# Order of the four matmul groups inside one attention score tile of a two-layer block

## The chip, the cores and the metric

The kernel runs on one core of a Trainium2 chip. The metric is the time on the device, in microseconds (us), from launch to end, as the median of several runs. Smaller is better. Instructions run on five engines side by side: TensorE (PE; its weight loads are listed as PEld), VectorE (DVE), ScalarE (ACT), GpSimd (POOL) and SyncE (SP), which only issues transfers.

## The reference, cut to what matters

The program is a block of two layers on x of shape (8, 512, 256). The change lies in the attention of the first layer, with 16 heads of 64 dimensions:

```python
q = _rmsnorm((x @ Wq).reshape(B, T, H, D), q_rms_w)
k = _rmsnorm((x @ Wk).reshape(B, T, H, D), k_rms_w)
v = (x @ Wv).reshape(B, T, H, D)
gate = softplus(einsum('bthd,hd->bht', k, u_n) / sqrt(D))
dist = maximum(idx[:, None] - idx[None, :], 0)
bias = -dist[None, None] * omega_eff[None, :, None, None] * gate[:, :, None, :]
bias = where(causal[None, None], bias, -inf)
scores = einsum('bihd,bjhd->bhij', q, k) * scale + bias
attn = softmax(scores, axis=-1)
y = einsum('bhij,bjhd->bihd', attn, v).reshape(B, T, H * D)
return y @ Wproj
```

The rest of the block (layer norms, an expert layer with routing, a small two-matrix layer and a block-sparse feed-forward layer) is untouched. Scores are a sum of three terms: q by k, a bias linear in the distance, and a causal mask.

## The kernel before, in words

**Stages.** A first stage (until about 137 us of the span) normalises and transposes all eight sequences and routes tokens to experts. The middle stage (137 to 1283 us) holds attention, the output projection and the experts. The last (to the end) is the second layer.

**Attention.** It runs over 32 groups: eight sequences times four groups of four heads. For each group `produce` projects q and k (L456), v and the gate (L464), scales and transposes q and k (L514), and builds the gate rows gT (L639 and its copy at L646). Then `attend(u)` runs over 256 units: 64 pairs of heads times four blocks of 128 query rows, taken in the order 2, 0, 3, 1. Block i looks at w = 128(i + 1) key columns, so that units have 384, 128, 512 and 256 columns.

**One unit.** `scores` fills a PSUM tile `sc` of two banks, one bank for each head of the pair. Head 0 has its operands on partitions 0 to 63 and head 1 on 64 to 127, so a matmul of one head uses half of the array's rows (64*128 in the profile), and the two heads can run side by side. The three terms are accumulated in PSUM by four groups of matmuls, each of one matmul per head:

- the bias rows, L678: constant rows `bst` (bf16) as weights, `gT` (bf16) moving, w columns. The bias is carried by a few rows of each half;
- the mask in two groups, L683: constant selectors `mst` (bf16) as weights and large negative steps `mmv` (bf16) moving. The first (c = 0) covers the 128 columns of the diagonal block, the second (c = 1) its last 64 columns;
- q by k, L688: q transposed (fp32) as weights and k transposed (fp32) moving, w columns. Every fp32 matmul appears in the profile as two records.

The group that comes first has `start=True`, which overwrites what was in the bank; the last has `stop=True`.

After the scores, VectorE takes the row maximum (L694), ScalarE the exponentials with row sums (L700), VectorE the reciprocal (L707), GpSimd the division (L710), TensorE the transposes of the result, full-array matmuls of 128 columns (L723), and ScalarE and VectorE copy those out (L731, L733). After four units of a pair, TensorE multiplies by v (L756). `output` (L786) projects finished sequences.

**What sets the order.** A planner written in the kernel (`Plan`) decides the order. Each operation states its engine, a cost in ns, what it depends on, a due time, and which buffers it takes and returns. `emit` simulates the engines with these costs and calls the functions in the order that results; each engine then runs its own queue in that order. All ten score matmuls of one unit are a single operation:

```python
sc = op("PE", 110 + 270 * (i + 1), scores, s.ready, u, acq=["sc"], rel=last, mode="R")
```

Its mode is "R" (half of the rows); other TensorE operations have "F" (full array), "C" (half of the columns) or "E" (experts), and the planner adds 93 ns where the mode changes. There are two score buffers (`sc`). A unit's scores need the group's gT and transposed q and k (`s.ready`), and a free score buffer, returned by the second exponential.

**Elsewhere in the profile.** In the last layer, L1195 is an fp32 matmul that uses 64 rows (64*128) of 256 columns between full-array matmuls of L1197, and L1183 is a bf16 matmul on 16 rows (16*128) of 512 columns between full-array fp32 matmuls of L1179.

Of the kernel before, what the change touches and what calls it, by code (L numbers as in the profile page):

```python
# [139 lines left out]
def tile_two_layer_block(  # L140
# [26 lines left out]
    nc = tc.nc  # L167
# [27 lines left out]
    bst = const.tile([P, NPR, T], BF16, tag="bst", name="bst")  # L195
# [4 lines left out]
    for h in range(2):  # L200
        k = slice(h * D, (h + 1) * D)
# [96 lines left out]
    with tc.tile_pool(name="pa", bufs=2) as pa, tc.tile_pool(name="pa1", bufs=1) as pa1:  # L298
# [13 lines left out]
        for half in range(B // BPG):  # L312
            lg = sc_tile(f"lg_{half}")
            xns = []
            for i in range(BPG):
# [11 lines left out]
                for dc in range(NC):  # L327
                    nc.tensor.matmul(
                        lg[i * E : (i + 1) * E, :], gwT[:, dc, :], xT[:, dc, :],
                        start=(dc == 0), stop=(dc == NC - 1),  # L330
# [38 lines left out]
            for i in range(BPG):  # L369
                for dc in range(NC):  # L370
                    col = (i * NC + dc) * E
                    for t in range(NT):
# [4 lines left out]
                            start=(t == 0), stop=(t == NT - 1),  # L377
# [50 lines left out]
    with tc.tile_pool(name="pb", bufs=2) as pb, tc.tile_pool(name="pb1", bufs=1) as pb1:  # L428
# [231 lines left out]
        def attend(u):  # L660

            pr, c = divmod(u, NT)
            n, q = divmod(pr, NPR)
            i = ORDER[c]
            s = grp[n]
            n0 = i * P
            w = n0 + P
# [4 lines left out]
            m = Grp()  # L672
            heads = [(h, slice(h * D, (h + 1) * D)) for h in range(2)]

            def scores():
                m.sc = ps_sc.tile([P, 2, T], F32, tag="sc", name=f"sc_{u}")
                for h, k in heads:
                    nc.tensor.matmul(  # L678
                        m.sc[:, h, :w], bst[k, q, n0:w], s.gT[k, :w], start=True, stop=False
                    )  # L680
                for c in range(2):
                    for h, k in heads:
                        nc.tensor.matmul(  # L683
                            m.sc[:, h, n0 + c * D : w], mst[k, c, :], mmv[k, c, c * D :],
                            start=False, stop=False,
                        )
                for h, k in heads:
                    nc.tensor.matmul(  # L688
                        m.sc[:, h, :w], s.qT[k, q, n0:w], s.kT[k, q, :w], start=False, stop=True
                    )  # L690

            def most():
                m.nm = pb.tile([P, 2], F32, tag="nmx", name=f"nm_{u}", bufs=3)
# [40 lines left out]

            last = ["qk", "gT"] if u % NU == NU - 1 else []
            sc = op("PE", 110 + 270 * (i + 1), scores, s.ready, u, acq=["sc"], rel=last, mode="R")
            mx = op("DVE", 69 + 2.07 * w, most, [sc], u + 0.1, acq=["nm"])
            e0 = op("ACT", 254 + 0.83 * w, lambda: expo(0), [mx], u + 0.2, acq=[f"pr{i}", "sums"])
# [228 lines left out]
    with tc.tile_pool(name="pc", bufs=2) as pc, tc.tile_pool(name="pc1", bufs=1) as pc1:  # L967
# [98 lines left out]
        for dc in range(NC):  # L1066
            for k in range(NC):
# [3 lines left out]
                    start=(k == 0), stop=(k == NC - 1),  # L1071
# [177 lines left out]
```

## Time and profile before

| | |
|---|---|
| median of 3 runs | 1664.84 us (1663.77 to 1667.19) |
| profiled execution | 1665.2 us, its span 1663.5 us |
| mean granted TensorE clock | 0.977 |
| TensorE busy, 0 to 137 us | 91.33 us |
| TensorE busy, 137 to 1283 us | 1132.63 of 1146.00 us |
| TensorE busy, 1283 to 1663.5 us | 369.15 of 380.50 us |
| score matmuls L688: records, busy | 1024, 201.0 us |
| mask matmuls L683: records, mean | 512 of 128 columns, 216 ns; 512 of 64 columns, 189 ns |
| bias matmuls L678: records, mean by columns | 128 each: 225 ns (128), 279 (256), 333 (384), 386 (512) |

How to read it: the span runs from the first to the last instruction of one profiled execution. A line such as "L678 PE MATMUL sc<-gT,bst 64*128 64x384 bf16" names the source line, the engine, the output and its inputs, the part of the array in use (rows*columns), and the moving operand (rows x columns and type). Lengths of matmul records are modelled and overlap with the following ones, since the array is pipelined: the distance from one start to the next is what TensorE really spends. LDWEIGHTS records are the loads of weights into the array, which can lie beside a running matmul.

### The profile page before, as it was taken

To read this page: it belongs to the slowest core of one execution; us is meant where nothing else is said; L and a number is where in the kernel's file an instruction comes from. 1 tells how busy PE (TensorE), PEld (TensorE's weight loads), DVE (VectorE), ACT (ScalarE), POOL (GpSimd) and SP (SyncE) were. 2 spreads that over 40 slices of the span, in tenths; PEclk is the share of its full clock that TensorE was granted. 3 is DMA by queue.
4 is the path that set the end of the run, shared out by engine and by line. 5 is a ranking of instruction groups with operands and counts; after the bars stand their busy time and mean duration, and the time that the engine had idled before them with its cause. 6 is when DMAs were issued, how large, how long until landed. Compare 5 with 4: busy or idle time off the path is not lost.

```text
span 1663.5 us, 26380 instructions
## 1 busy us (share of the span) xinstructions
PE 1593.1 (96%) x9416; PEld 933.3 (56%) x9416; DVE 922.3 (55%) x2682; ACT 700.5 (42%) x1918; POOL 590.7 (36%) x1082
## 2 busy tenths in 40 slices
PE   4789999999999999999999999999999899999999
PEld 1455555655665565565556556655655655555555
DVE  5537666666666665665666676666666332333331
ACT  1115554455446544544555454455545121222221
POOL 4016444444444444534444444444444100000000
PEclk9679999999999999999999999999999899999999
DMA  8000113032011302211130122123014000000000
GB/s 267 26 4 1 52 53 106 8 105 81 30 58 52 103 11 81 77 57 58 52 103 7 58 79 80 46 67 103 7 58 138 14 10 13 14 13 13 13 13 16
DMA packets 72914, 89.26 MB, mean 54 GB/s; under 512 B 5016, under 2 KB 55984, under 8 KB 72784
## 3 DMA queue, kind: packets, MB, share of 16 engines
q1 hardware_dynamic: 71552, 86.87, 16.0%
q8 instruction: 75, 1.23, 0.3%
q10 hardware_dynamic: 1232, 0.71, 0.2%
q14 instruction: 55, 0.45, 0.1%
HBM read 83.11 MB, written 4.19 MB: 52 GB/s over the span
## 4 chain that ended last, share of the span: by engine, by line
PE 89%; DVE 3%; ACT 1%; issue 1%; POOL 0%; ACTq 0%; DVEq 0%; POOLq 0%
PE pq L456 13%; PE sc L688 9%; PE pp L723 9%; PE y L756 9%; PE ph L1179 7%; PE py L1197 7%; PE po L786 7%; PE pv L464 6%; PE pqk L514 4%; PE sc L678 4%; PE peo L925 2%; PE ph L867 2%; PE sc L683 1%; PE ph L1183 1%; PE py L1195 1%; PE ph L861 1%
## 5 line engine op out<-in xcount | busy, mean ns | idle before, releaser
L710 POOL TENSOR_SCALAR pr<-pr,rinv 128x384 f32<-128x384 f32 (+3 forms) x512 | 265.9, 532 | 424.8 <-DVE rinv L707 244.3
L700 ACT ACTIVATE pr<-sc,nm 128x384 f32<-128x384 f32 (+3 forms) x512 | 266.2, 527 | 139.3 <-DVE nm L694 73.9
L241 POOL TENSOR_TENSOR rsqk<-ss,nhalf 128x8 f32<-128x8 f32 x128 | 210.8, 1647 | 146.5 <-DVE ss L491 140.9
L456 PE MATMUL pq<-wqk_sb,xnT 128*128 128x512 f32 x512 | 247.4, 606 | 3.3 <-DVE gl L482 3.3
L694 DVE TENSOR_REDUCE nm<-sc 128x2 f32<-128x768 f32 (+3 forms) x256 | 209.8, 823 | 73.4 <-PE sc L688 70.7
L723 PE MATMUL pp<-ident,pr 128*128 128x128 f32 x1280 | 218.9, 281 | 4.9 <-DVE prT L733 2.7
L723 PEld LDWEIGHTS pp<-ident,pr 128*128 128x128 f32 x1280 | 147.7, 141 | 122.0 <-issue 60.0
L688 PE MATMUL sc<-kT,qT 64*128 64x384 f32 (+3 forms) x1024 | 201.0, 471 | 0.0
L731 ACT COPY prT<-pp 128x384 f32<-128x384 f32 (+3 forms) x256 | 107.2, 426 | 156.4 <-PE pp L723 154.5
L733 DVE COPY prT<-pp 128x384 f32<-128x384 f32 (+3 forms) x256 | 123.4, 487 | 84.2 <-PE pp L723 81.2
L756 PE MATMUL y<-prT,v 128*64 128x256 f32 (+3 forms) x1024 | 152.2, 439 | 0.7 <-ACT prT L731 0.7
L464 PE MATMUL pv<-wvg_sb,xnT 128*128 128x260 f32 x512 | 136.4, 389 | 8.0 <-DVE osb L938 6.8
L456 PEld LDWEIGHTS pq<-wqk_sb,xnT 128*128 128x128 f32 x512 | 87.9, 192 | 85.3 <-issue 70.7
L1179 PE MATMUL ph<-xT,w1T 128*128 128x512 f32 x256 | 128.7, 620 | 0.0
L756 PEld LDWEIGHTS y<-prT,v 128*64 128x64 f32 x1024 | 68.4, 136 | 105.0 <-issue 63.4
L1197 PE MATMUL py<-w2T,hT 128*128 128x256 f32 x512 | 124.0, 388 | 0.0
L786 PE MATMUL po<-wp_sb,yT 128*128 128x256 f32 x512 | 116.4, 381 | 0.0
L1105 POOL TENSOR_TENSOR xres<-x,b_bc 128x1024 f32<-128x1024 f32 x8 | 18.8, 2344 | 265.1 <-DVE x L1098 265.1
L471 ACT ACTIVATE sq<-pq 128x512 f32<-128x512 f32 x128 | 76.3, 596 | 81.4 <-PE pq L456 78.6
L464 PEld LDWEIGHTS pv<-wvg_sb,xnT 128*128 128x128 f32 x512 | 89.0, 191 | 36.8 <-issue 14.6
L1197 PEld LDWEIGHTS py<-w2T,hT 128*128 128x128 f32 x512 | 93.3, 190 | 25.7 <-issue 15.3
L488 DVE TENSOR_REDUCE ss<-sq 128x8 f32<-128x512 f32 x128 | 87.4, 683 | 35.7 <-ACT sq L471 34.9
(187 smaller groups left out, 2067.7 us busy)
## 6 DMA issues: line engine op xcount, KB each, us to landing
ew<-in_L_ffn_w_dram SPq DMA_DIRECT2D x128, 512.0 KB
xt<-in_L_attn_x_dram SPq DMA_DIRECT2D x8, 512.0 KB
xr<-in_L_attn_x_dram SPq DMA_DIRECT2D x32, 128.0 KB
out_dram<-ot SPq DMA_DIRECT2D x32, 128.0 KB
raw<-in_L_ffn_w_dram SPq DMA_DIRECT2D x4, 512.0 KB
wqk_sb<-in_L_attn_Wq_dram SPq DMA_DIRECT2D x2, 512.0 KB
wqk_sb<-in_L_attn_Wk_dram SPq DMA_DIRECT2D x2, 512.0 KB
wvg_sb<-in_L_attn_Wv_dram SPq DMA_DIRECT2D x2, 512.0 KB
```

Source lines behind the costliest of these rows:

```text
L241: nc.gpsimd.tensor_tensor(r, src, nhalf[:, :n], ALU.pow)
L456: nc.tensor.matmul(s.pq[t], xnT[b][:, dc, cols], wqk_sb[:, dc, g, :], start=(dc == 0), stop=(dc == NC - 1),)
L464: nc.tensor.matmul(s.pv[t][:, : GW + HG], xnT[b][:, dc, cols], wvg_sb[:, dc, g, :], start=(dc == 0), stop=(dc == NC - 1),)
L688: nc.tensor.matmul(m.sc[:, h, :w], s.qT[k, q, n0:w], s.kT[k, q, :w], start=False, stop=True)
L694: nc.vector.tensor_reduce(m.nm, m.sc[:, :, :w], AX.X, ALU.max, negate=True)
L700: nc.scalar.activation(m.p[:, h, :], m.sc[:, h, :w], AF.Exp, bias=m.nm[:, h : h + 1], accum_out=m.sums[:, h : h + 1],)
L710: nc.gpsimd.tensor_scalar(m.p[:, h, :], m.p[:, h, :], m.rinv[:, h : h + 1], 1.0, ALU.mult, ALU.mult)
L723: nc.tensor.transpose(m.pt[h][:, d * P : (d + 1) * P], m.p[:, h, j * P : (j + 1) * P], ident)
L756: nc.tensor.matmul(pp.yp[h * D : (h + 1) * D, j * P :], s.v[j][:, hh * D : (hh + 1) * D], pp.tri[:, h, j : j + 4 * (NT - 1 - j) + 1 : 4, : ...
L786: nc.tensor.matmul(o.po[:, :C], yT[b * nk + k][:, t * P : (t + 1) * P], wp_sb[:, k, :], start=(k == 0), stop=(k == nk - 1),)
L1179: nc.tensor.matmul(ph, w1T[:, dc, k * P : (k + 1) * P], s.xT[:, dc, :], start=(dc == 0), stop=False,)
L1197: nc.tensor.matmul(py[:, :C], hT[:, c, cols], w2T[:, c, :], start=False, stop=(c == NFC - 1),)
```

## The change

Inside `scores` the order of the groups becomes q by k, first mask (c = 0), bias rows, second mask (c = 1). `start=True` moves to q by k, and `stop=True` to the second mask. The operands, the shapes and the number of matmuls stay as they are, and so do the operation's cost, due time, mode and buffers in the planner, and with them the order of operations on every engine. Later lines have their numbers raised by two.

```diff
                 for h, k in heads:
                     nc.tensor.matmul(
-                        m.sc[:, h, :w], bst[k, q, n0:w], s.gT[k, :w], start=True, stop=False
+                        m.sc[:, h, :w], s.qT[k, q, n0:w], s.kT[k, q, :w], start=True, stop=False
                     )
                 for c in range(2):
                     for h, k in heads:
                         nc.tensor.matmul(
                             m.sc[:, h, n0 + c * D : w], mst[k, c, :], mmv[k, c, c * D :],
-                            start=False, stop=False,
-                        )
-                for h, k in heads:
-                    nc.tensor.matmul(
-                        m.sc[:, h, :w], s.qT[k, q, n0:w], s.kT[k, q, :w], start=False, stop=True
-                    )
+                            start=False, stop=bool(c),
+                        )
+                    if c == 0:
+                        for h, k in heads:
+                            nc.tensor.matmul(
+                                m.sc[:, h, :w], bst[k, q, n0:w], s.gT[k, :w],
+                                start=False, stop=False,
+                            )
```

## The prediction, made before the changed kernel ran

> **What bounds the kernel now.** I read the busy shares first, then the chain that ended last, then TensorE's waits inside the attention stage, and last single matmuls there in order of time. From the page, parts 1 and 4:
>
> ```profile
> span 1663.5 us, 26380 instructions
> PE 1593.1 (96%) x9416; PEld 933.3 (56%) x9416; DVE 922.3 (55%) x2682; ACT 700.5 (42%) x1918; POOL 590.7 (36%) x1082
> ...
> PE 89%; DVE 3%; ACT 1%; issue 1%; POOL 0%; ACTq 0%; DVEq 0%; POOLq 0%
> ```
>
> TensorE holds 89% of the chain, and the other engines have slack. The scores run from 137 to 1283 us. In the table of that one stretch TensorE is busy 1132.63 of 1146.00 us, at a granted clock of 1.00, so what one score unit takes on TensorE goes into the end time almost unabated. The view of TensorE's waits in this stretch has two lines that concern this change:
>
> ```profile
> PE pv L464 <- DVE osb L938: 6.8, 7, 1.0
> PE sc L678 <- ACT pr L700: 1.5, 4, 0.4
> ```
>
> The columns are total us, times and longest. Score units wait 1.5 us in all, always for a score buffer to come free; they never wait for the bias rows gT. Starting with q by k can therefore save no wait.
>
> Now one unit of 384 columns, in order of time (start us, length us; "x2" are the two heads, which run side by side in the two halves of the array):
>
> ```profile
> 613.71 0.27 PE L723 MATMUL pp<-ident,pr 128*128 128x128 f32 x1
> 613.92 0.34 PE L678 MATMUL sc<-gT,bst 64*128 64x384 bf16 x2
> 614.09 0.25 PE L683 MATMUL sc<-mmv,mst 64*128 64x128 bf16 x4
> 614.17 0.57 PE L688 MATMUL sc<-kT,qT 64*128 64x384 f32 x2
> 614.58 0.49 PE L688 MATMUL sc<-kT,qT 64*128 64x384 f32 x2
> 615.00 0.70 PE L464 MATMUL pv<-wvg_sb,xnT 128*128 128x260 f32 x2
> ```
>
> Lengths are modelled and overlap, so I count from start to start, and below use the trace's start stamps to the nanosecond. Each fp32 matmul has two records. The first q by k record lasts 0.57, the second 0.48 (0.49 in this merged line): something holds up the first. The view of weight loads in the same stretch shows it:
>
> ```profile
> 613.91 0.10 PEld L678 LDWEIGHTS <-bst 64*128 64x128 bf16 x2 [0.17 <-issue]
> 613.93 0.26 PEld L683 LDWEIGHTS <-mst 64*128 64x128 bf16 x4
> 614.15 0.30 PEld L688 LDWEIGHTS sc<-kT,qT 64*128 64x128 f32 x4
> ```
>
> The fp32 load for q by k starts at 614.15, when the last mask matmul has only just begun. That matmul streams 27 ns, so most of the load stands uncovered. The bias load starts only at 613.91, 0.20 us after the last transpose began, although it was next in the queue: at the passage from the full array to half arrays nothing is loaded ahead.
>
> **What the skill says.** TensorEngine Tiling (Array Packing), section Key Properties: changing the tiling mode drains the engine. The trace agrees: 613.71 to 613.916 is 205 ns where two transposes in a row start 107 ns apart, so 98 are lost; from the last q by k record to the next full-array matmul it is 413 ns against a streaming time of 320, that is 93, or 97 counted from the first head of the pair. TensorE: Matmul & The Clock Gate, section LDWEIGHTS: a load takes its columns over 1.2, which for 128 is 107 ns; the first fp32 matmul after a passage is 104 to 107 ns longer than the second throughout this trace. The same page, Weight-path perf modes: the fast load is for 128 weights that aren't fp32. Here the bf16 bias record of 128 columns has a mean of 225 ns against 216 for a mask record of the same form, so its uncovered load costs about 10. The same page, Back-to-back issue gap: columns over 2.4. In this trace bf16 transposes of 128 start 55.5 ns apart, and an fp32 record counts twice.
>
> **The change part by part.** No instruction is added or removed: ten matmul records per unit, in the order q by k, first mask, bias, second mask. Pure streaming stays 2x2w + w + 128 + 64 columns, 880 ns for w = 384, and cancels. What lies around it changes. Before, bias start to next start is 549, 813, 1080 and 1346 ns (medians for 128, 256, 384, 512 columns); less streaming of 347, 613, 880 and 1147, that leaves 200 to 202, with these parts (ns):
> - 13, first load (bias, bf16) and the second head's offset;
> - 3 from mask to mask, 2 from mask to q by k;
> - 86, q by k's load behind the 27 ns mask (the 0.57 against 0.48);
> - 97, drain to the next step.
> With the 98 of the drain on entry it is 298.
>
> After:
> 1. Entry drain. Full to half array with fp32 first is in the trace at the last layer's L1195 (64*128, 256 columns): 309 ns from the L1197 before it, less 213, gives 96. So 2 less.
> 2. First load, now q by k's fp32 one: the same L1195 shows it uncovered.
>
> ```profile
> L1195 PE MATMUL py<-aw2T,gT x64: 376/428/480, 1338.0 to 1656.3; 64*128 64x256 f32 x64
> ```
>
> 480 is the first record and 376 the second. From first to second start it is 320 ns, less 213: 107 where the bias load cost 13.
>
> 3. q by k's load behind a mask goes: 86 to 0.
> 4. q by k to first mask, mask to bias, bias to second mask: 3 each. The mask's bf16 load lies behind a q by k record of at least 107 ns, the bias load behind a 53 ns mask and the second mask's behind the bias. From fp32 to bf16 inside half-array mode no record exists; in full mode it is 109 against 107 (transpose to bf16 transpose), so I take 3. If this passage isn't free, see the second rival.
> 5. Drain to the next step after a bf16 mask. The trace has L1183 (16*128 bf16, 512 columns), 314 to the next start, less 213, less its own uncovered load of 13: 88, and 3 for the second head make 91. With nothing taken off it is 101, with the second head 104. I take 94, plus 2 for the 27 ns matmul ahead. The next step's load stays uncovered before and after, since the passage loads nothing ahead; that the step before it is now short costs nothing.
> Sum: 96 + 107 + 9 + 2 + 94 = 308, so 10 ns more per visit, with ends 305 (+7) and 318 (+20).
>
> The plan's order has two units in succession ten times, where only the first pays for the entry and the second's q by k hides behind a short mask as before. So 256 units make 246 visits: 246 x 10 = 2.5 us, ends 1.7 and 4.9.
>
> **Others who are touched.** The operations' order on every engine is the same, for costs and due times in the plan are unchanged; no DMA moves. The buffer wait (1.5 us) passes to the first q by k record, and the wait for gT, at a group's first unit, to the bias behind it: behind both stands only TensorE's own queue, and neither was ever late by more than the 0.4 shown. The maximum on VectorE starts when the last record of the unit is written, some 10 ns later; its own idle time before TensorE's scores doesn't hold the chain.
>
> The profiled execution took 1665.2 us (span 1663.5 and 1.7 around it), the median shown is 1664.84. So 1665.2 + 2.5 = 1667.7 for such an execution, and 1667.3 on the scale of the medians. A measurement of this kernel can't tell less than about 0.2%, 3.3 us, from no change.
>
> **Rivals.**
> - *The load of q by k goes ahead during the drain* (faster). Then the 107 are gone: 246 x 97 = 23.9 us less than before, 1641. For it: it would be a different load from the bias's. Against it: L1195 after full-array work, and every first fp32 record of the other modes (pv at 615.00 lasts 0.49 where later ones last 0.38). A smaller gain through gT's late arrival has no wait to live on.
> - *fp32 to bf16 in half-array mode isn't seamless* (slower). At the place q by k to first mask, the mask's load might not be hidden: 13 ns x 256 = 3.3 us, together 1670.6. If the passage drains as a mode change does, 96 x 256 = 24.6 us, together 1691.9. It decides from about 4 ns per unit on, since 0.8 us more brings the sum to 3.3. For it: no record shows the passage. Against it: the full-array one at 2 ns.
> - *The exit after a short bf16 matmul is the dear one*: the upper end above, 246 x 20 = 4.9, 1669.7; it is in the forecast's own range.
>
> **How the numbers follow.** The forecast, a trade of one uncovered load for another at 1666.5 to 1669.7, has a chance of 0.70, of which 0.48 are within 0.2%, 0.20 slower, 0.02 faster by scatter. The second rival has 0.20 (0.15 small, 0.05 a full drain), 0.19 of it slower and 0.01 within. The first has 0.10, with unforeseen gains: 0.08 faster, 0.02 within. Sum: faster 0.10, same 0.51, slower 0.39. The time is 1667.3. The range leaves out the full drain and the gain of a hidden load: 1663.7 to 1671.5, with about 2 us of the scatter shown (1663.77 to 1667.19) at either end.
>
> **What would show it.** In the new profile's first unit: the q by k pair directly after the 0.20 us gap, its first record about 105 ns longer than the second (0.59 and 0.48 at 384 columns); the bias record of 384 columns down from 333 by some 10; unit start to next start about 1092 at 384. Step 4 is wrong if q by k's second record to the mask takes over 325 ns at 384 columns, step 5 if second mask to next start is outside 118 to 134, step 2 if both q by k records are alike. If TensorE's waits in the stretch 137 to 1283 us change from 13 us by more than 2, the reason isn't on TensorE, and the forecast misses it.

## The result, and the profile after

| | before | changed |
|---|---|---|
| median, first comparison (7 runs each) | 1664.98 us | 1670.41 us |
| ratio | | 1.0031 (1.0019 to 1.0043) |
| median, second comparison (59 and 22 runs) | 1666.56 us | 1670.20 us |
| ratio | | 1.0023 (1.0014 to 1.0032) |
| profiled execution, span | 1663.5 us | 1668.1 us |

The change makes the kernel slower by 0.2 to 0.3%: 5.4 us in the first set of runs, 3.6 us between the medians of the second and larger one. The forecast was 1667.3 us; the time is inside the range and the direction of the 2.5 us was right, but it is more than what had been summed. By the forecast's own line of 0.2%, no change had the larger chance (0.51, against 0.39 for slower): the first comparison lies beyond this line, and the second, at 0.23% (0.14 to 0.32), isn't clear of it.

The page of the changed kernel, parts 1 and 4:

```profile
span 1668.1 us, 26384 instructions
PE 1597.7 (96%) x9416; PEld 953.1 (57%) x9416; DVE 921.9 (55%) x2682; ACT 700.5 (42%) x1918; POOL 590.8 (35%) x1082
...
PE 89%; DVE 3%; ACT 1%; issue 1%; POOL 0%; ACTq 0%; DVEq 0%; POOLq 0%
```

TensorE has 4.6 us more busy time, and the span is 4.6 us longer. The weight loads (PEld), which can lie beside a matmul, take 19.8 us more; the other engines' busy times are the same within 0.4 us. TensorE's waits in the stretch 137 to 1283 us (total us, times, longest):

```profile
PE pv L464 <- DVE osb L940: 6.8, 7, 1.0
...
PE sc L678 <- ACT pr L702: 1.2, 3, 0.4
```

They are those of before, and the score buffer's wait has passed to q by k. So the time has gone into TensorE's own work. The unit of 384 columns that the prediction took apart, now in the changed kernel, as the timeline shows it, matmuls first and weight loads below:

```profile
614.69 0.27 PE L725 MATMUL pp<-ident,pr 128*128 128x128 f32 x1
614.90 0.59 PE L678 MATMUL sc<-kT,qT 64*128 64x384 f32 x2
615.32 0.49 PE L678 MATMUL sc<-kT,qT 64*128 64x384 f32 x2
615.64 0.22 PE L683 MATMUL sc<-mmv,mst 64*128 64x128 bf16 x2
615.70 0.33 PE L689 MATMUL sc<-gT,bst 64*128 64x384 bf16 x2
615.86 0.20 PE L683 MATMUL sc<-mmv,mst 64*128 64x64 bf16 x2
615.99 0.71 PE L464 MATMUL pv<-wvg_sb,xnT 128*128 128x260 f32 x2
```

```profile
614.89 0.30 PEld L678 LDWEIGHTS sc<-kT,qT 64*128 64x128 f32 x4 [0.16 <-issue]
615.32 0.10 PEld L683 LDWEIGHTS <-mst 64*128 64x128 bf16 x2
615.65 0.10 PEld L689 LDWEIGHTS <-bst 64*128 64x128 bf16 x2 [0.22 <-issue]
615.70 0.10 PEld L683 LDWEIGHTS <-mst 64*128 64x128 bf16 x2
615.99 0.52 PEld L464 LDWEIGHTS pv<-wvg_sb,xnT 128*128 128x128 f32 x3 [0.18 <-DVE ss L488]
```

The first fp32 load starts at 614.89, together with its matmul and not with the transpose before it: all of it lies open, that is, no matmul runs beside it, and the first q by k record takes 0.59 us. The masks' and the bias's loads start while a matmul runs ahead of them; from start to start only 2 to 3 ns are added to the streaming in this unit. From the first start to the next step's start it is now 1094 ns where it was 1080; at 128, 256 and 512 columns the medians are 563, 827 and 1360 where they were 549, 813 and 1346.

Laid over each other operation by operation, the two traces show where the 4.6 us arise. The score visits are 3.54 us longer in sum (246 x 14.4 ns), and the transposes, most of which lead into them, 0.72 us shorter (those of L723 0.62, those of q and k 0.10). Together 2.82 us. The beginning of the last layer adds 0.28 us, and the first stage is 0.20 us shorter. Another 1.69 us come at one place in the last layer, which the change doesn't touch. The table of stages shows this place for the 4 us around it in the changed kernel (us, then busy time of PE, PEld, DVE, ACT, POOL, then the granted clock, DMA share, GB/s):

```profile
1414.00:1418.00 4.00, 4.00 (x11) 2.96 (x11) 2.09 (x17) 1.22 (x2) 0.00 (x0) 0.57 0.00 0
```

The granted clock is at half for 3.4 us there, which is 1.7 us lost. The same work in the profile before, which comes 3 to 5 us earlier, lies within these 12 us and ran at a clock of 1.00:

```profile
1405.40:1417.40 12.00, 12.00 (x59) 8.37 (x58) 4.19 (x23) 1.54 (x2) 0.00 (x0) 1.00 0.07 23
```

### The profile page after: what moved, and what is told of

The parts are those of the page before. It is cut to its first block, busy times and chain, and to the rows that moved or that the text cites. A ratio compares the mean times of both kernels' runs of the same rounds, so it can differ in the third digit from the quotient of the medians.

```text
span 1668.1 us, 26384 instructions
## 1 busy us (share of the span) xinstructions
PE 1597.7 (96%) x9416; PEld 953.1 (57%) x9416; DVE 921.9 (55%) x2682; ACT 700.5 (42%) x1918; POOL 590.8 (35%) x1082
## 4 chain that ended last, share of the span: by engine, by line
PE 89%; DVE 3%; ACT 1%; issue 1%; POOL 0%; ACTq 0%; DVEq 0%; POOLq 0%
PE pq L456 13%; PE sc L678 11%; PE pp L725 9%; PE y L758 9%; PE ph L1181 7%; PE py L1199 7%; PE po L788 7%; PE pv L464 6%; PE pqk L514 4%; PE sc L689 2%; PE peo L927 2%; PE ph L869 2%; PE sc L683 1%; PE ph L1185 1%; PE py L1197 1%; PE ph L863 1%
## 5 line engine op out<-in xcount | busy, mean ns | idle before, releaser
L678 PE MATMUL sc<-kT,qT 64*128 64x384 f32 (+3 forms) x1024 | 207.1, 481 | 1.4 <-ACT pr L702 1.4
```

Of the source, the lines that this page charges most:

```text
L678: nc.tensor.matmul(m.sc[:, h, :w], s.qT[k, q, n0:w], s.kT[k, q, :w], start=True, stop=False)
```

## The experiments

Two questions were open: whether the half-clock stretch belongs to the change, and whether the score units' part comes from uncovered weight loads, as summed, or from something else in the new order (the change from fp32 to bf16, the bias behind a short mask, the exit after a short matmul). All kernels below compute the same sums in another order of the four groups. In all of them `start=True` stands at the first group and `stop=True` at the last. The edits are shown against the kernel before, cut to the lines that say where a group stands.

**Both kernels once more, in one set of runs on one chip.**

The kernel before:

> The kernel before once more, as its own comparison. Theory A (the change costs only what its score units show, 12 ns on each of 246 visits, 2.9 us; the rest of the 5.4 us measured is one more stretch of 3.4 us at half clock in the last layer, 1.7 us, that comes or stays away by chance of phase): 1664 to 1667, a ratio of 1.000, and some of its runs with a mean clock of 0.976 and a span about 1.7 us above those with 0.977. Theory B (the change itself brings the half-clock stretch or another cost outside the score units): all of its runs at 0.977, spans within 1 us.

The changed kernel:

> The changed kernel once more. Theory A: spans with clock 0.977 about 1666.3 to 1667.3, those with 0.976 about 1.7 us more; runs of equal clock 2.9 us, to 3.8 us, above the kernel before. Theory B: nearly all at 0.976, and a difference above 4.5 us also at equal clock.

Measured: 1666.52 us for the repeated kernel before, ratio 0.9999 (0.9991 to 1.0007); 1670.20 for the changed one, ratio 1.0023. Sorted by each run's mean clock:

| mean clock | before (59 runs) | changed (22 runs) | difference |
|---|---|---|---|
| 0.975 | 1667.94 (6 runs) | 1669.91 (2) | 1.97 |
| 0.976 | 1667.03 (33) | 1670.39 (12) | 3.36 |
| 0.977 | 1665.63 (6) | 1668.63 (2) | 3.00 |
| 0.980 and 0.981, against 0.982 | 1662.13 (14) | 1664.93 (3) | 2.80, but the clocks aren't equal |

Three more runs of the changed kernel lie at 0.974 (1673.55 and 1674.19) and 0.972 (1675.47); none of the 59, nor of the 22 of the repeated kernel before, is under 0.975.

A stretch of 3.4 us at half clock lowers the mean over 1665 us by 0.001, and costs 1.7 us where TensorE never waits. At equal clock, as far as three digits show it, 2.0 to 3.4 us remain, the 2.0 from two runs alone. That is near the 3.1 of the score visits, their transposes and the beginning of the last layer.

What Theory B expected of the kernel before isn't so: its repeated runs lie at 0.976 (12 runs, 1666.95 us), 0.977 (5, 1665.66) and 0.981 (5, 1662.26), so that other clocks come without the change too. But the change isn't cleared of the stretch at 1414 us. It stands at this place in two of the four traces of kernels that begin with q by k, and in none of the four that begin with the bias. The repeated kernel before was profiled at 0.976 without it: there the clock from 20 to 50 us is 0.73 where it was 0.76, and 1.36 of the 1.55 us by which its span is longer arise before 137 us. So the place that Theory A names, the last layer, isn't the rule for the kernel before. Whether the order of the groups makes the stretch at 1414 us more likely stays open.

The repeated changed kernel was profiled at 0.977, with a clock of 1.00 from 1405 to 1425 us. Its score visits are 3.54 us longer once more, and the transposes 0.72 shorter. Its span is 3.9 us above that of the profile before, at the same mean clock: 2.8 us in the middle stage, 0.3 at the beginning of the last layer, and 0.7 in the first stage, which the change doesn't touch.

**Bias first, then q by k, then both masks.** The changed lines:

```diff
-                for c in range(2):
-                    for h, k in heads:
-                        nc.tensor.matmul(
-                            m.sc[:, h, n0 + c * D : w], mst[k, c, :], mmv[k, c, c * D :],
...
-                        m.sc[:, h, :w], s.qT[k, q, n0:w], s.kT[k, q, :w], start=False, stop=True
+                        m.sc[:, h, :w], s.qT[k, q, n0:w], s.kT[k, q, :w], start=False, stop=False
...
+                        m.sc[:, h, n0 : w], mst[k, 0, :], mmv[k, 0, :],
+                        start=False, stop=False,
...
+                        m.sc[:, h, n0 + D : w], mst[k, 1, :], mmv[k, 1, D:],
+                        start=False, stop=True,
```

> Order bias, q by k, first mask, second mask: it has the passage from fp32 to bf16 and the exit after a short bf16 mask, as the changed kernel has, but starts with the quick bf16 load, and the fp32 load lies behind the bias record. Account of uncovered loads (107 ns less what the matmul ahead streams): 13 at the start; q by k's load uncovered by 54 ns at 128 columns, by 0 at 256, 384, 512. Units shorter than before by about 27 ns at 128 columns and 81 at the others: start to next start about 522, 732, 999, 1265 ns; 64 x (27 + 3 x 81) = 17.3 us less, about 1647.7, ratio 0.990. Rival (the cost of the change lies in the passage from fp32 to bf16 or in the exit after a short matmul, not in the first load): it remains slower than before or equal, 1665 to 1668.

Measured: 1649.45 us, ratio 0.9896 (0.9883 to 0.9909). Start to next start is 522, 733, 997 and 1264 ns; the score visits are 17.28 us shorter in sum, where 17.3 were expected. The rival falls: this order has both the passage from fp32 to bf16 and the short last matmul, and is 1% faster than the kernel before. The same unit in its trace, matmuls and loads:

```profile
606.75 0.27 PE L727 MATMUL pp<-ident,pr 128*128 128x128 f32 x1
606.96 0.34 PE L678 MATMUL sc<-gT,bst 64*128 64x384 bf16 x2
607.13 0.48 PE L682 MATMUL sc<-kT,qT 64*128 64x384 f32 x2
```

```profile
606.96 0.36 PEld L682 LDWEIGHTS sc<-kT,qT 64*128 64x128 f32 x4
```

q by k's load starts at 606.96 with the bias matmul, 0.17 us ahead of its own matmul, and the first q by k record takes 0.48, as the second does. The groups by form show where the cover is too short (the figures are busy us and mean ns of a q by k record; first the kernel before, then this one):

```profile
L688 PE MATMUL sc<-kT,qT 64*128 64x512 f32 x256 | 70.8, 630 | 0.0
L688 PE MATMUL sc<-kT,qT 64*128 64x128 f32 x256 | 29.9, 312 | 0.0
```

```profile
L682 PE MATMUL sc<-kT,qT 64*128 64x512 f32 x256 | 65.4, 589 | 0.0
L682 PE MATMUL sc<-kT,qT 64*128 64x128 f32 x256 | 28.2, 298 | 0.0
```

At 512 columns the mean is 589, the length of the second record alone, where it was 630. At 128 it is 298, where an unhindered record has 272: half of 53, since only the first of two records waits.

**Bias, first mask, q by k, second mask.**

```diff
-                for c in range(2):
-                    for h, k in heads:
-                        nc.tensor.matmul(
-                            m.sc[:, h, n0 + c * D : w], mst[k, c, :], mmv[k, c, c * D :],
...
-                        m.sc[:, h, :w], s.qT[k, q, n0:w], s.kT[k, q, :w], start=False, stop=True
+                        m.sc[:, h, n0 : w], mst[k, 0, :], mmv[k, 0, :],
...
+                        m.sc[:, h, :w], s.qT[k, q, n0:w], s.kT[k, q, :w], start=False, stop=False
...
+                        m.sc[:, h, n0 + D : w], mst[k, 1, :], mmv[k, 1, D:],
+                        start=False, stop=True,
```

> Order bias, first mask, q by k, second mask: the fp32 load of q by k lies behind a mask of 128 columns (53 ns) where the kernel before has one of 64 (27 ns). Account of uncovered loads: 107 - 53 = 54 uncovered, with the pair's offset 57 or so, where it was 86 behind 27 ns; the exit after a bf16 mask is 2 to 3 dearer. Units 27 to 30 ns shorter than before at every width: about 521, 785, 1052, 1318 ns, together 6.9 to 7.4 us less, ratio 0.9957. Rival (a load behind any short mask is lost alike, and what helped the order with q by k second was only the number of changes between formats): units as before within 5 ns, ratio 1.000.

Measured: 1659.64 us, ratio 0.9957 (0.9943 to 0.9971). Start to next start is 522, 786, 1053 and 1319 ns; in sum 6.78 us less than before, where the medians of the runs are 6.3 us apart. The rival falls. The groups by form of this kernel:

```profile
L687 PE MATMUL sc<-kT,qT 64*128 64x512 f32 x256 | 69.0, 617 | 0.0
L687 PE MATMUL sc<-kT,qT 64*128 64x128 f32 x256 | 28.2, 298 | 0.0
```

617 against 589 and 298 against 272: 26 to 28 on the mean, so 53 to 56 ns on the first record at either width. What lies open is set by the matmul just ahead, not by the unit's size.

**q by k, bias, then both masks.**

```diff
-                        m.sc[:, h, :w], bst[k, q, n0:w], s.gT[k, :w], start=True, stop=False
...
+                        m.sc[:, h, :w], s.qT[k, q, n0:w], s.kT[k, q, :w], start=True, stop=False
...
-                        m.sc[:, h, :w], s.qT[k, q, n0:w], s.kT[k, q, :w], start=False, stop=True
+                        m.sc[:, h, :w], bst[k, q, n0:w], s.gT[k, :w], start=False, stop=False
...
+                        m.sc[:, h, n0 : w], mst[k, 0, :], mmv[k, 0, :],
+                        start=False, stop=False,
...
+                        m.sc[:, h, n0 + D : w], mst[k, 1, :], mmv[k, 1, D:],
+                        start=False, stop=True,
```

> Order q by k, bias, first mask, second mask: the bias is moved behind q by k, the rest as in the changed kernel. Account of uncovered loads: the first load costs 107 as in the changed kernel, every later one is hidden; units equal to the changed kernel's within 3 ns (563, 827, 1094, 1360), time within 1 us of it. Rival (the bias behind a 53 ns mask pays for its place): units 10 to 13 ns shorter, 2.5 to 3.3 us less than the changed kernel.

Measured: 1669.98 us, ratio 1.0020 (1.0012 to 1.0027); at a clock of 0.976 it is 1670.10 (16 runs) against the changed kernel's 1670.39. The medians of the units are 563, 827, 1094 and 1360, the same as the changed kernel's to the nanosecond. The bias's place behind the short mask costs nothing.

**q by k, both masks, bias last.**

```diff
-                        m.sc[:, h, :w], bst[k, q, n0:w], s.gT[k, :w], start=True, stop=False
...
+                        m.sc[:, h, :w], s.qT[k, q, n0:w], s.kT[k, q, :w], start=True, stop=False
...
-                        m.sc[:, h, :w], s.qT[k, q, n0:w], s.kT[k, q, :w], start=False, stop=True
+                        m.sc[:, h, n0 : w], mst[k, 0, :], mmv[k, 0, :],
...
+                        m.sc[:, h, n0 + D : w], mst[k, 1, :], mmv[k, 1, D:],
...
+                        m.sc[:, h, :w], bst[k, q, n0:w], s.gT[k, :w], start=False, stop=True
```

> Order q by k, first mask, second mask, bias: as the changed kernel, but the last matmul before the exit is the bias with all its columns in place of a mask of 64. Account of uncovered loads: units as in the changed kernel within 3 ns (563, 827, 1094, 1360), since nothing is loaded ahead at the exit and the first load costs 107 as there. Rival (a short last matmul makes the exit dear): units 5 to 10 ns shorter than the changed kernel's, most at 512 columns.

Measured: 1670.67 us in a single run, at a clock of 0.975, so that only its trace is used. Units of 563, 827, 1094 and 1360 again, although the last matmul has up to 512 columns. Its end at 384 columns:

```profile
618.30 0.33 PE L692 MATMUL sc<-gT,bst 64*128 64x384 bf16 x2
618.56 0.49 PE L464 MATMUL pv<-wvg_sb,xnT 128*128 128x260 f32 x1
```

From the bias to the next step it is 260 ns, 160 of streaming and 100; at the other widths 100 to 101 are left, and behind the changed kernel's mask 100. The exit doesn't depend on the length of the last matmul, so the shortness of the changed kernel's last mask isn't what made it slower.

The three orders that begin with q by k have the same median unit times, whatever follows. The three that begin with the bias differ in time by what stands ahead of q by k, to within 2 ns. The open part is counted from the start of the first q by k record to that of the second, less the streaming; beside it stands the account, 107 ns less what the matmul ahead streams:

| matmul ahead of q by k | it streams, ns | account, ns | open part, ns |
|---|---|---|---|
| none (mode has just changed) | 0 | 107 | 106 to 107 |
| second mask, 64 columns | 27 | 80 | 86 |
| first mask, or bias of 128 columns | 53 | 54 | 58 to 59 |
| bias of 256 columns or more | 107 and up | 0 | 2 to 5 |

Behind another matmul the open part is 2 to 6 ns above the account. What makes up these few ns was not tried.

## Why the prediction was right, and what it missed

**The bound and the waits**: right. The chain is TensorE's as before, no wait of TensorE's changed by more than 0.3 us in the score stretch, and the wait for gT was indeed never late.

**The sums.** The parts listed before the change add to 201 ns, and to 299 with the entry, where 298 stands; the rests without streaming are 199 to 202, not 200 to 202. Nothing hangs on 1 ns. One reading of the trace goes too far: not every first fp32 matmul after a passage is 104 to 107 ns longer than the next. The fp32 transposes (L723, L514) are 56 ns longer there, 165 ns from start to start where two in a row have 109. Why theirs is shorter wasn't tried; q by k behaves like L1195, from which its 107 was taken. And what is quoted from the section Back-to-back issue gap leaves out its last term: the Trainium skill, TensorE: Matmul & The Clock Gate, adds 2.5 ns per matmul there, and the 2 to 3 ns from matmul to matmul in the unit of 384 columns agree.

**Step 1, entry drain** (2 less): right in direction; from the last transpose to the first score matmul it is 202 to 203 ns instead of 205.

**Step 2, the first load** (107 for 13): right. 427 ns from the first to the second q by k record at 384 columns, less 320. The bias record of 128 columns fell from 225 to 216 on average, the length of a mask:

```profile
L689 PE MATMUL sc<-gT,bst 64*128 64x128 bf16 x128 | 14.2, 216 | 0.0
```

**Step 3, the load behind the mask** (86 to 0): right, and shown by the two orders that keep the bias first and change what covers that load.

**Step 4, the hand-overs** (3 each): measured 2, 3 and 2 at 384 columns. From fp32 to bf16 in half-array mode it is 322 ns from the second q by k record to the mask, 2 above streaming (5 at 128 columns). The second rival, which put 13 or 96 ns there, was wrong.

**Step 5, the exit** (94 and 2): this is the term that was mis-sized. From the second mask to the next step it is 127 ns, 27 of streaming and 100; it lay inside the band of 118 to 134, but 4 above what was taken. Behind an fp32 first load the two heads start 6 to 7 ns apart and not 3, and that offset is carried to the end of the unit. Where the bias comes first the offset stays at 3, and the same passage, from the second mask to the next step, takes the 123 ns that had been summed: so the term was short by the offset, not by the drain.

With it the sum of step 1 to 5 is 96 + 107 + 7 + 100 = 310 where 308 were forecast, against 298 before: 12 ns per visit and not 10, so 2.9 us by the sum and 2.82 in the traces. The count of 246 visits was right.

**The step from this to the time** is where the forecast fell short of the first measurement. It took the span of one profiled execution, with its clock of 0.977, as the scale for both kernels, and gave about 2 us at either end for scatter. The first set's difference of 5.4 us is above the 4.9 at the upper end of the sum: that it lies inside the range is owed to this allowance, not to the account of the units. The first set of the changed kernel's runs had a clock of 0.976 in six of seven, its profile a 3.4 us half-clock stretch that the profile before had not. At equal clock the larger set gives 2.0 to 3.4 us, 0.12 to 0.20%: within what had been called no change, or at its edge. The profile of the order q by k, bias, masks has such a stretch at the same place (1414.6 us), those of the changed kernel's repetition and of the order with the bias last have none. Why it comes in one execution and stays away in another isn't settled; nothing was tried on it. The 0.3 us at the beginning of the last layer (0.28 in this trace, 0.33 in the repetition) arise where the clock passes from half to full; that was not followed further.

**The first rival** (a load that goes ahead during the drain) was wrong: the load starts with its matmul, at 614.89.

## What to carry to other kernels

Where matmuls of different weight types share one stay in a tiling mode, begin with those whose weights load fast, and put the slow load behind a matmul that streams at least as long as the load takes: in this kernel that is worth 1.0% (1649.45 us), with nothing else altered, where the order studied here cost 0.2 to 0.3%. Count the open loads of a sequence one by one, first member included, since a mode change leaves the first one open; the number of format changes and the length of the last matmul did not matter here. For differences of a few us, compare runs of equal mean clock, and look where the clock was low: from 0.977 (1665.63 us) to 0.981 (1661.94) the kernel before gained 3.7 us, where four stretches at 1.7 would make 6.8.

## What the runs showed of the hardware

- The Trainium skill, TensorEngine Tiling (Array Packing), section Key Properties, states the drain at a change of mode; the runs add that weights weren't loaded ahead across it, in either direction (614.89 and 615.99, each with its matmul), and that the drain, counted from the first head of a pair, was 96 to 101 ns in these units for fp32 and bf16 alike.
- The bias's load of 128 bf16 weights cost about 10 to 13 ns where it lay open, q by k's of 128 fp32 weights 107. Between the order bias, q by k, masks and those that begin with q by k, a unit differs by 94 to 97 ns at 256 columns and more, and by 41 at 128.
- TensorE's clock fell to half for 3.4 us at 1414 to 1418 us while its busy time was full (4.00 of 4.00 us). A busy PE in the page is no sign of a full clock.
